# A branch over the last four chunks of three expert mixtures, and scatters moved to other places, in an eight-layer graph network

## The chip, the core and the metric

The kernel runs on one core of one Trainium2 chip. The core has five engines that run beside each other: PE (TensorE, matrix products), DVE (VectorE), ACT (ScalarE), POOL (GpSimd) and SP (SyncE, which here only starts transfers). PE's loading of weights is listed as PEld. Each engine works through its own instructions in order and waits on semaphores for the others. Data stand in on-chip memory as 128 partitions; PE's results go to a smaller accumulation memory and are copied out. Transfers to and from device memory (DMA) are started by SP, by ACT, or by POOL where the addresses come from an index list (an indirect DMA: a gather or a scatter of one row per partition).

The metric is the device time of one execution, in microseconds (us), median over several runs. A profile is taken of one execution, whose own time can differ a little from the median.

## The reference, cut to what matters

A state x of 3125 nodes by 256 features goes through eight steps; each adds its result to x, and each but the first works on a layer norm of x.

```
x = L0_gnn(x)                 # weighted sum over edges
x = x + L0_ffn(norm(x))       # mixture: 8 experts, hidden 512, top 2, relu
x = x + L1_gnn(norm(x))       # two attention passes over 50000 edges + self loops, 4 heads
x = x + L1_ffn(norm(x))       # mixture: 8 experts, hidden 256, top 2, gelu
x = x + L2_gnn(norm(x))       # weighted graph convolution and two dense layers
x = x + L2_ffn(norm(x))       # attention over 65536 edges, then 4 small experts, top 2
x = x + L3_gnn(norm(x))       # mean over neighbours, two layers
x = x + L3_ffn(norm(x))       # mixture: 8 experts, hidden 1024, top 2, gelu
```

The mixtures of L0, L1 and L3 are alike. For L0:

```
gate_logits = x_flat @ Wg + bg + bias
topk_vals, topk_idx = jax.lax.top_k(gate_logits, 2)
topk_w = jax.nn.softmax(topk_vals, axis=-1)
combine = (jax.nn.one_hot(topk_idx, 8) * topk_w[..., None]).sum(axis=1)
h = jax.nn.relu(jnp.einsum('td,edh->teh', x_flat, W1) + b1)
y = jnp.einsum('teh,ehd->ted', h, W2) + b2
out = jnp.einsum('ted,te->td', y, combine)
```

Only the two chosen experts of a node count, so 2 x 3125 = 6250 rows have to go through an expert. The attention passes of L1_gnn need, for each edge, the source node's projected row and a softmax over the edges of each target node. L2_ffn attends over another, larger edge list of its own.

## The kernel before, in words

The nodes are T = 25 tiles of 128; the state X stays on the chip. Most per-node work goes by groups of TG = 5 tiles. The steps are listed in FAST_STEPS (line 2523): `clear`, `r0_gnn`, `take_edges`, `middle`, `r2_gnn`, `r2_ffn`, `r3_gnn`, `r3_ffn`; `middle` (line 2325) holds L0's mixture, L1's attention and L1's mixture. A function `look` runs first and sorts the edges; it writes a flag that tells whether the fast way fits the data. All of the steps stand inside one branch on that flag (line 2534), the kernel's only one. Each engine loads the flag and branches for itself.

A planner orders the instructions of a stretch without branches (a basic block) on each engine, by program order and its own estimates of time. `in_order` (line 1919) takes that choice away: it chains all instructions of the engines named, in program order. Inside `middle` POOL is in order; in `attend` PE, DVE and ACT are too.

**A mixture** is `gated` (line 861). Before it the router has placed each node's row, for each of its two choices, into a device-memory buffer `regions`, which has one region for each expert (POOL scatters, line 831). `gated` counts each expert's rows, rounds up to chunks of CH = 256 rows (`gd_nch`), and takes the running sum over the experts (`gd_end`); the last entry of this sum is the number of chunks in use. Since no loop bound depends on the data, it runs as many chunks as could ever be needed, K = (2*3125 + 8*255)//256 = 32. A chunk k (lines 939 to 970) is: SP reads the chunk's expert and row from a table; loads the 256 rows (gx_xs), the expert's weights and its second bias; PE transposes the rows (L955); DVE copies them (L957); PE multiplies by the first weights (L962), ACT applies the function (L963); PE multiplies by the second weights (L933), one chunk later in program order; DVE adds the bias (L935); ACT stores 256 rows of results (L936) into `ff_results`. Chunks past the last one in use compute with expert 7 on rows that nobody reads. Afterwards (lines 972 to 978), for each tile and each of the two choices, POOL gathers the result rows (gb_y, through `gather`, L322) and DVE multiplies by the gate weight and adds into X (L977): 50 gathers, through 6 buffers.

**L1's attention** is `r1_gnn` (line 2255). It starts the next mixture's router (`mix_start`, line 712, with two small POOL iotas, L721 and L727, and DVE's `gd_zero`, L730), loads the head weights (`head_weights`, line 1905: the load hw_w at L1910, then DVE L1915 and L1916 twice each), and then, for each group of five tiles, normalises (`norm_group`: DVE L150, L156, L157; ACT L160; DVE L162, L163, five small ones and L170) and computes the `heads` (PE transposes, ACT L1942, PE L1946, ACT L1948, SP store of r_rows L1949, three small DVE operations). The second pass's weights use the same buffer, so their load waits until the last heads matmul has read the first ones. Then come two passes of `attend`. Each gathers 416 blocks of 128 edges' rows (POOL L322, ad_rows<-r_rows) and works on them; the second pass's gathers read what the first pass's last tiles stored.

**Scatters for L2_ffn.** The 65536 edges of L2_ffn are put in place by 512 POOL scatters (`own_send`, line 1733, instruction L1737: os_table<-os_rec), which are spread over the earlier steps wherever `own_send(n, after)` is called; each call issues the next n scatters, no earlier than the instruction `after`. The calls before: 4 after each of the first five buckets filled in L0_gnn (line 1474), two in each iteration of its main loop, 3 in each chunk of L0's and of L1's mixture (line 965; 96 each), 40 in `r1_gnn` after the head weights (line 2270), and `tail` (line 2297) with 6 a call, four calls at the end of each attention pass. What is left goes after L1's mixture. All 512 must be done before L2_ffn.

`rank_edges`, part of `look`, ranks the edges in their blocks; its PE matmuls are L1316, in three groups.

Of the kernel before, what the change touches and what calls it, by code (L numbers as in the profile page):

```python
# [61 lines left out]
class Net:  # L62
    def __init__(self, ctx, tc, a):
        self.ctx, self.tc, self.nc, self.a = ctx, tc, tc.nc, a
        self.turn = 0
# [27 lines left out]
    def clear(self):  # L93

        v = self.regions.rearrange("(q p r) d -> q p r d", p=P, r=8)
        for q in range(v.shape[0]):
            self.nc.sync.dma_start(v[q], self.zero[:, None, 0:D].to_broadcast([P, 8, D]))

# [762 lines left out]
    def gated(self, m, w1, b1, w2, b2, act, beside=None, send=0):  # L861
# [11 lines left out]
        K = (2 * N + E * (CH - 1)) // CH  # L873
        with tc.tile_pool(name="ge", bufs=1, side=m.side) as pool:
# [9 lines left out]
            nc.vector.tensor_tensor_scan(end, nch, nch, 0.0, OP.add, OP.max)  # L884
            kk = pool.tile([P, K], F32, name="gd_kk")
# [29 lines left out]
            with tc.tile_pool(name="gx_w", bufs=2) as wp, tc.tile_pool(name="gx_x", bufs=2) as xp, \  # L915
# [22 lines left out]
                last = None  # L938
                for k in range(K):

                    with tc.issue_after(prev.ins) if k else nullcontext():
                        e = nc.sync.value_load(ci[0:1, 0, k:k + 1], min_val=0, max_val=E - 1)
                        r = nc.sync.value_load(ci[0:1, 1, k:k + 1], min_val=0, max_val=E * RC - CH)
                    xs = xp.tile([P, CJ, D], F32, name="gx_xs")
                    nc.sync.dma_start(xs, regions[bass.ds(r, CH), :].rearrange("(j p) d -> p j d", p=P))
                    w1s = wp.tile([P, DC, F], F32, name="gx_w1")
                    nc.sync.dma_start(w1s, a[w1][bass.ds(e, 1), :, :].rearrange("o (c p) f -> p (o c) f", p=P))
                    w2s = wp.tile([P, FC, D], F32, name="gx_w2")
                    nc.sync.dma_start(w2s, a[w2][bass.ds(e, 1), :, :].rearrange("o (c p) d -> p (o c) d", p=P))
                    b2s = wp.tile([P, D], F32, name="gx_b2")  # L950
                    prev = nc.sync.dma_start(b2s, a[b2][bass.ds(e, 1), :].rearrange("o d -> (o d)").partition_broadcast(P))
                    pt = pt_.tile([P, DC, CH], F32, name="gx_pt")
                    for j in range(CJ):
                        for c in range(DC):
                            nc.tensor.transpose(pt[:, c, j * P:(j + 1) * P], xs[:, j, c * P:(c + 1) * P], self.ident)  # L955
                    xt = xp.tile([P, DC, CH], F32, name="gx_xt")
                    nc.vector.tensor_copy(xt, pt)  # L957
                    h = hp.tile([P, FC, CH], F32, name="gx_h")
                    for f in range(FC):
                        ps = pa_.tile([P, CH], F32, name="gx_pa")  # L960
                        for c in range(DC):
                            nc.tensor.matmul(ps, w1s[:, c, f * P:(f + 1) * P], xt[:, c, :], start=c == 0, stop=c == DC - 1)  # L962
                        done = nc.scalar.activation(h[:, f, :], ps, act, bias=bias1[:, f, k:k + 1])  # L963
                    if send:
                        self.own_send(send, done)
                    if last:
                        second(*last)
                    if beside and k == 1:
                        beside()
                    last = (k, h, w2s, b2s)  # L970
                second(*last)
            with tc.tile_pool(name="gb", bufs=6) as bp:
                for t in range(T):
                    for i in range(2):
                        y = bp.tile([P, D], F32, name="gb_y")
                        self.gather(y, results, at[i][:, t:t + 1])
                        nc.vector.scalar_tensor_tensor(self.X[:, t, :], y, w[i][:, t:t + 1], self.X[:, t, :],  # L977
                                                       op0=OP.mult, op1=OP.add)
# [179 lines left out]
class Fast(Net):  # L1158
# [114 lines left out]
    def rank_edges(self, over):  # L1273
# [4 lines left out]
        with tc.tile_pool(name="re", bufs=1) as pool, tc.tile_pool(name="re_ps", bufs=2, space=PSUM) as psp:  # L1278
# [31 lines left out]
            for i, (u, v, kb) in enumerate(((0, 12, KB), (12, T - 1, KB), (T - 1, T, KL))):  # L1310
# [3 lines left out]
                for j in range(2):  # L1314
                    for k in range(kb):
                        nc.tensor.matmul(ps[:, j, 0:n].rearrange("p (d s) -> p d s", s=T), both[:, j, :], hv[:, k],  # L1316
                                         start=k == 0, stop=k == kb - 1)
# [105 lines left out]
    def r0_gnn(self):  # L1423
# [12 lines left out]
        with ExitStack() as ctx:  # L1436
# [34 lines left out]
            for d in range(G):  # L1471
                for _ in self.fill_bucket((bp, psb), f5, d):
                    pass
                self.own_send(4, self.filled)
# [445 lines left out]
    def in_order(self, *engines):  # L1920

        tc, bb = self.tc, self.nc.cur_bb.bb
        n = len(bb.instructions)
        yield
        assert self.nc.cur_bb.bb is bb
        engines = [e.engine for e in engines]
        prev = {}
        for i in list(bb.instructions)[n:]:
            if i.engine in engines:
                if i.engine in prev:  # L1930
# [324 lines left out]
    def r1_gnn(self):  # L2255
# [7 lines left out]
        with tc.tile_pool(name="r1", bufs=1) as pool, tc.tile_pool(name="r1_ps", bufs=1, space=PSUM) as psp:  # L2263
# [33 lines left out]
            def tail(i):  # L2297
                self.own_send(6, i)
# [273 lines left out]
```

## Time and profile before

| what | value |
|---|---|
| median of 3 runs | 5167.04 us (5164.95 to 5167.39) |
| profiled execution, its own time | 5171.12 us |
| its span, first to last instruction | 5169.1 us |
| mean granted TensorE clock | 0.831 |
| busy: PE, DVE, ACT, POOL | 69%, 56%, 40%, 40% of the span |
| L0's chunks, 745 to 992 us of the span | 247 us |
| L0's 50 gathers, 996 to 1060 | 64 us |
| from there to the first attention gather, at 1132 | 72 us |
| L1's chunks, 2394 to 2556 | 162 us |
| L3's chunks, 4630 to 5095 | 465 us |

In the profile's timeline a row is: start in us from the beginning of the span, duration in us, engine, line of the kernel, operation, output<-inputs by the program's names, shapes, the count of merged instructions, and in brackets how long the engine had been idle before and what released it ("issue": nothing that the profile shows). "PE gx_pa L962 x32" in the chain is a piece of the chain that ended last, with its start and length. In "1024.0 KB" DMA rows and elsewhere buffer numbers are left out of names.

### The profile page before, as it was taken

How to read it: one execution, taken by the hardware profiler on the slowest of the kernel's cores; microseconds unless marked ns; L12 is line 12 of the kernel's file. 1: busy time of each engine (PE TensorE's matmuls, PEld its weight loads, DVE VectorE, ACT ScalarE, POOL GpSimd, SP SyncE). 2: the span in 40 equal slices, each digit the busy share in tenths (PEclk: the TensorE clock that was granted, in tenths of full speed). 3: DMA queues.
4: the chain of work that ended last, by engine and by line, in shares of the span. 5: the costliest groups of instructions: out<-in, count | busy, mean ns of one | idle time of the engine just before them, and what ended most of it. 6: DMA issues, size and time to landing. Idle time of an engine off the chain costs nothing.

```text
span 5169.1 us, 67040 instructions
## 1 busy us (share of the span) xinstructions
PE 3584.2 (69%) x21332; PEld 2847.3 (55%) x21332; DVE 2916.1 (56%) x9571; ACT 2087.0 (40%) x5715; POOL 2063.2 (40%) x2082
## 2 busy tenths in 40 slices
PE   1399969625666354554648876168786999979994
PEld 1399958524444243443537754035554788868883
DVE  7998842255666466663358874577747872231112
ACT  3466432116666467661129961023232331112220
POOL 0365443467776677775620000777700000120003
PEclk9699979866777677777969986578887999989997
DMA  1632237534554344434723311111100112225554
GB/s 55 206 109 103 99 123 234 174 89 136 142 142 125 97 133 130 135 99 132 205 74 115 115 57 45 34 31 35 33 1 25 68 68 76 92 103 193 193 192 135
DMA packets 345199, 562.37 MB, mean 109 GB/s; under 512 B 69987, under 2 KB 255719, under 8 KB 341637
## 3 DMA queue, kind: packets, MB, share of 16 engines
q1 hardware_dynamic: 229050, 373.88, 21.8%
q0 software_dynamic: 84032, 154.27, 11.7%
q10 hardware_dynamic: 31754, 29.84, 1.7%
q8 instruction: 172, 2.82, 0.2%
q14 instruction: 191, 1.56, 0.1%
HBM read 412.89 MB, written 145.37 MB: 108 GB/s over the span
## 4 chain that ended last, share of the span: by engine, by line
PE 44%; POOL 11%; DVE 9%; ACT 9%; issue 8%; DMA 5%; SPq 1%; DVEq 0%; ACTq 0%; POOLq 0%
POOL ad_rows L322 9%; PE gx_pa L962 7%; PE r_pa L1581 7%; PE gx_po L933 7%; PE ad_acc L2133 6%; ACT oo_y L1801 4%; PE q_a L2484 3%; PE q_o L2492 3%; PE r_o L1596 2%; DMA ad_rows<-r_rows,fa_gi 1%; DMA gb_y<-ff_results,gd_at 1%; ACT ad_rows L2123 1%; ACT oo_hp L1802 1%; ACT oo_h L1802 1%; DMA gx_xs<-regions 1%
## 5 line engine op out<-in xcount | busy, mean ns | idle before, releaser
L322 POOL DMA_INDIRECT ad_rows<-r_rows,fa_gi x832 | 823.3, 990 | 266.4 <-issue 241.3
L1737 POOL DMA_INDIRECT os_table<-os_rec,os_at x512 | 531.1, 1037 | 526.2 <-ACT gx_h L963 194.0
L322 POOL DMA_INDIRECT ad_rows<-q_rows,own_gi x416 | 402.6, 968 | 719.9 <-DMA q_rows<-q_hx 593.4
L2123 ACT ACTIVATE ad_rows<-ad_rows 128x64 f32<-128x64 f32 x2544 | 617.0, 334 | 1.6
L2133 PE MATMUL ad_acc<-ad_rows,ad_hd 128*128 128x260 f32 x1664 | 515.9, 464 | 3.3 <-ACT ad_rows L2123 2.4
L831 POOL DMA_INDIRECT regions<-gh_xn,gd_at x150 | 157.5, 1050 | 845.7 <-PE r_o L1596 624.4
L1581 PE MATMUL r_pa<-r_xs,r_cnt 128*128 128x257 bf16 x3750 | 467.7, 277 | 28.1 <-DVE r_xs L1357 14.2
L963 ACT ACTIVATE gx_h<-gx_pa,gx_bias 128x256 f32<-128x256 f32 x448 | 211.9, 473 | 671.2 <-PE gx_pa L962 642.6
L935 DVE TENSOR_TENSOR gx_ys<-gx_po,gx_b 128x256 f32<-128x256 f32 x192 | 80.6, 423 | 622.1 <-PE gx_po L933 600.8
L962 PE MATMUL gx_pa<-gx_xt,gx_w 128*128 128x256 f32 x1792 | 418.5, 388 | 6.8 <-DMA gx_w<-in_L_ffn_W 3.2
L933 PE MATMUL gx_po<-gx_w,gx_h 128*128 128x256 f32 x1792 | 419.5, 380 | 0.0
L1581 PEld LDWEIGHTS <-r_cnt 128*128 128x128 bf16 x3750 | 365.0, 99 | 84.9 <-issue 29.4
L2133 PEld LDWEIGHTS ad_acc<-ad_rows,ad_hd 128*128 128x128 f32 x1664 | 365.8, 232 | 68.9 <-ACT ad_rows L2123 5.4
L2036 PE MATMUL ad_pt<-ident,ad_e 128*4 128x128 f32 x75 | 26.6, 354 | 525.9 <-DVE ad_e L2033 396.0
L962 PEld LDWEIGHTS gx_pa<-gx_xt,gx_w 128*128 128x128 f32 x1792 | 336.6, 192 | 81.7 <-DVE gx_xt L957 21.5
L933 PEld LDWEIGHTS gx_po<-gx_w,gx_h 128*128 128x128 f32 x1792 | 331.2, 190 | 44.0 <-ACT gx_h L963 2.6
L322 POOL DMA_INDIRECT gb_y<-ff_results,gd_at x150 | 144.3, 962 | 526.9 <-DMA ff_results<-gx_ys 476.1
L2036 PEld LDWEIGHTS ad_pt<-ident,ad_e 128*4 128x4 f32 x75 | 6.1, 82 | 559.1 <-issue 527.4
L1462 PE MATMUL r_pa<-r_xn,r_wt 128*128 128x257 f32 x1250 | 298.1, 383 | 7.2 <-ACT r_wt L1497 5.9
L2360 PE MATMUL ss_sum<-r_xw,ss_wt 128*128 128x256 f32 x1250 | 292.0, 396 | 6.3 <-DMA ss_wt<-mats 6.3
L2360 PEld LDWEIGHTS ss_sum<-r_xw,ss_wt 128*128 128x128 f32 x1250 | 246.9, 199 | 42.3 <-issue 6.7
L1462 PEld LDWEIGHTS r_pa<-r_xn,r_wt 128*128 128x128 f32 x1250 | 228.4, 192 | 35.5 <-ACT r_wt L1497 6.5
(555 smaller groups left out, 6920.6 us busy)
## 6 DMA issues: line engine op xcount, KB each, us to landing
gx_w<-in_L_ffn_W SPq DMA_DIRECT2D x64, 1024.0 KB
mats<-r_wt SPq DMA_DIRECT2D x25, 1600.0 KB
ss_wt<-mats SPq DMA_DIRECT2D x25, 1600.0 KB
gx_w<-in_L_ffn_W SPq DMA_DIRECT2D x64, 512.0 KB
regions<-zero SPq DMA_DIRECT2D x26, 1024.0 KB
ad_rb<-fa_relT SPq DMA_DIRECT2D x48, 544.0 KB
gx_xs<-regions SPq DMA_DIRECT2D x96, 256.0 KB
ff_results<-gx_ys ACTq DMA_DIRECT2D x96, 256.0 KB
```

Source lines behind the costliest of these rows:

```text
L322: return self.nc.gpsimd.indirect_dma_start(out=out, out_offset=None, in_=table[:, :], in_offset=bass.IndirectOffsetOnAxis(ap=idx, axis=0))
L831: ins = nc.gpsimd.indirect_dma_start(out=self.regions[:, :], out_offset=bass.IndirectOffsetOnAxis(ap=m.at[i][:, t:t + 1], axis=0), in_=x, ...
L933: nc.tensor.matmul(po, h[:, f, j * P:(j + 1) * P], w2s[:, f, :], start=f == 0, stop=f == FC - 1)
L962: nc.tensor.matmul(ps, w1s[:, c, f * P:(f + 1) * P], xt[:, c, :], start=c == 0, stop=c == DC - 1)
L963: done = nc.scalar.activation(h[:, f, :], ps, act, bias=bias1[:, f, k:k + 1])
L1462: nc.tensor.matmul(pa, wt[:, i, :], xn[:, g * G + i, :], start=i == 0, stop=i == G - 1)
L1581: nc.tensor.matmul(pa, c[:, u, :], xs[i - 1][:, u, j, :], start=u == 0 and j == 0, stop=u == T - 1 and j == 2)
L1737: i = nc.gpsimd.indirect_dma_start(out=s.table[:, :], out_offset=bass.IndirectOffsetOnAxis(ap=s.at[:, c:c + 1], axis=0), in_=s.rec[:, c, : ...
L1801: nc.scalar.activation(y[:, k, :], self.iotab, AF.Abs, bias=minus[:, k:k + 1])
L2123: i = nc.scalar.activation(v, v, AF.Copy, scale=x.rt[:, k, W4 + h:W4 + h + 1])
L2133: nc.tensor.matmul(x.acc, lhs[:, k, :], rhs[:, k, :], start=i == 0, stop=i == x.kb - 1)
L2360: nc.tensor.matmul(sums[t], wt[:, d, :], rows[:, d, :], start=d == 0, stop=d == T - 1)
```

## The change

It does five things.

1. `gated` runs chunks 0 to KA - 1 = 27, with KA = 6250//256 + 8//2 = 28, as before. Chunks 28 to 31 stand in a branch that is taken when the number of chunks in use, loaded into a register of every engine, is above 28.
2. The result rows of these four chunks (1024 rows of 1 KB, 1 MB) are filled with zeros in each mixture, by one transfer that ACT starts in chunk 3.
3. The gathers of results become `mix_result`. For L0 they move into `r1_gnn`: for each group of five tiles ten gathers with their additions, then the group's norm and heads; ten gather buffers in place of six. The next mixture's `mix_start` comes after the heads.
4. Scatters: 7 after each of three matmul groups in `rank_edges` (new), 8 in place of 4 for each of the first five buckets, none in chunks 28 to 31, none of the 40 in `r1_gnn`, 9 in place of 6 in each call of the attention passes' tails.
5. `in_order` now works across basic blocks, by `resume`, `chain` and `branch`.

```
+    @contextmanager
+    def branch(self, cond):
+        for o in self.orders:
+            self.chain(o)
+        with self.tc.If(cond):
+            yield
+        for o in self.orders:
+            self.resume(o)
...
+        KA = (2 * N) // CH + E // 2
...
+            used = pool.tile([1, 1], I32, name="gd_used")
+            nc.vector.tensor_copy(used, end[0:1, E - 1:E])
...
-                    if send:
+                        if send and k < KA:
                             self.own_send(send, done)
...
+                        if k == 3:
+                            nc.scalar.dma_start(results[KA * CH:K * CH, :].rearrange("(q p) d -> p q d", p=P),
+                                                self.zero[:, None, 0:D].to_broadcast([P, (K - KA) * CJ, D]))
...
+                chunks(0, KA)
+                n = nc.values_load(used[0:1, 0:1], min_val=0, max_val=K)
+                with self.branch(n > KA):
+                    chunks(KA, K)
+        m.results = results
+        if tail:
             with tc.tile_pool(name="gb", bufs=6) as bp:
                 for t in range(T):
...
+                    self.mix_result(m, bp, t)
...
+    def mix_result(self, m, pool, t):
+        nc = self.nc
+        for i in range(2):
+            y = pool.tile([P, D], F32, name="gb_y")
+            self.gather(y, m.results, m.at[i][:, t:t + 1])
+            nc.vector.scalar_tensor_tensor(self.X[:, t, :], y, m.w[i][:, t:t + 1], self.X[:, t, :], op0=OP.mult, op1=OP.add)
...
+                self.own_send(7, done)
                 nc.vector.tensor_copy(start[:, u:v, :].rearrange("p d s -> p (d s)"), ps[:, 0, 0:n])
...
-                self.own_send(4, self.filled)
+                self.own_send(8, self.filled)
...
-            self.own_send(40)
             with tc.tile_pool(name="ln", bufs=2) as lp, tc.tile_pool(name="r1_xn", bufs=2) as xp, \
+                    tc.tile_pool(name="r1_h", bufs=3) as tp, tc.tile_pool(name="gb", bufs=10) as bp, \
                     tc.tile_pool(name="r1_p2", bufs=2, space=PSUM) as two:
                 for g in range(0, T, TG):
+                    for t in range(g, g + TG):
+                        self.mix_result(self.mix, bp, t)
                     xn = xp.tile([P, TG, D], F32, name="r1_xn")
                     self.norm_group(lp, xn, g)
...
+            self.mix_way.close()
+            self.mix_way = ExitStack()
+            m = self.mix = self.mix_start(self.mix_way, "L1_ffn_router_w", (), 8, probs=True, transpose=True, add=True)
...
-                self.own_send(6, i)
+                self.own_send(9, i)
```

## The prediction

> **What bounds the kernel now.** I read the page first, for the chain that ended last:
>
> ```profile
> PE 44%; POOL 11%; DVE 9%; ACT 9%; issue 8%; DMA 5%; SPq 1%; DVEq 0%; ACTq 0%; POOLq 0%
> POOL ad_rows L322 9%; PE gx_pa L962 7%; PE r_pa L1581 7%; PE gx_po L933 7%; PE ad_acc L2133 6%; ACT oo_y L1801 4%; PE q_a L2484 3%; PE q_o L2492 3%; PE r_o L1596 2%; DMA ad_rows<-r_rows,fa_gi 1%; DMA gb_y<-ff_results,gd_at 1%; ACT ad_rows L2123 1%; ACT oo_hp L1802 1%; ACT oo_h L1802 1%; DMA gx_xs<-regions 1%
> ```
>
> No one engine bounds it. The expert matmuls (L962 and L933, 14% together) and the attention gathers on POOL (L322, 9%) stand on the chain, and the change touches both. So I went stage by stage with a table of windows, one window for each loop over chunks (columns: busy us and instructions of PE, PEld, DVE, ACT, POOL; granted clock, DMA share, GB/s):
>
> ```profile
> 745.00:992.00 247.00, 245.70 (x1167) 205.96 (x1167) 57.74 (x147) 62.59 (x129) 93.24 (x96) 0.99 0.73 221
> 2394.00:2556.00 162.00, 138.30 (x640) 106.23 (x640) 46.64 (x96) 31.49 (x65) 90.84 (x94) 0.97 0.77 231
> 4630.00:5095.00 465.00, 464.10 (x2172) 399.95 (x2172) 48.40 (x95) 121.15 (x256) 0.00 (x0) 1.00 0.56 186
> ```
>
> PE is busy from end to end in L0 and L3, at a clock of 0.99 to 1.00; in L1 it is busy 138 of 162 us and waits for loads. Then the timeline around each edit.
>
> **Part 1: the skipped chunks, -107.9 us.** Each mixture sends two choices of 3125 nodes to 8 experts and runs K = 32 chunks of 256 rows. The branch runs chunks 28 to 31 only if more than 28 are used. That depends on the data, so I evaluated the reference's routing on its inputs. Rows per expert: L0 1325, 1693, 862, 239, 410, 1036, 474, 211; L1 522, 974, 433, 1344, 692, 713, 639, 933; L3 0, 1293, 416, 460, 1761, 84, 1429, 807. Rounded up to chunks each sums to 28 (L0: 6+7+4+1+2+5+2+1). 28 > 28 is false: all three are skipped. A count nearest to an upward flip is 1761, 31 rows below 1792; rounding won't move that. One chunk costs, by the starts of its transposes in L0 and of its L962 block in L3:
>
> ```profile
> 973.11 0.60 PE L955 MATMUL gx_pt<-ident,gx_xs 128*128 128x128 f32 x4
> 980.63 0.60 PE L955 MATMUL gx_pt<-ident,gx_xs 128*128 128x128 f32 x4
> ...
> 5060.21 7.11 PE gx_pa L962 x32
> 5067.32 6.04 PE gx_po L933 x28
> 5073.80 0.86 PE gx_po L933 x4
> 5074.66 7.11 PE gx_pa L962 x32
> ```
>
> 980.63 - 973.11 = 7.52 and 5074.66 - 5060.21 = 14.45. L1's first transposes start at 2394.53 and its last at 2549.84, 31 chunks later: 5.01. Four of each: 30.1 + 20.0 + 57.8 = 107.9.
>
> **Part 2: the branch itself, +1 us.** The only branch in the trace is the outer one, on the flag:
>
> ```profile
> 174.80 0.14 DVE L1243 TENSOR_SCALAR fa_flag<-fl_f 128x1 int32<-128x1 f32 x1
> 174.91 0.59 DVE L1343 TENSOR_TENSOR fa_rank<-re_r,re_r 128x416 bf16<-128x416 f32 x1
> 175.76 0.52 ACTq L921 DMA_DIRECT2D gx_b<-in_L_ffn_b  x1
> 175.82 0.14 POOL L721 IOTA gd_down<- 128x8 f32 x1 [135.19 <-DVE fa_rank L1343]
> ```
>
> From the flag written (174.94) to the first instruction behind it is 0.9 us, load and compare included, on the path that falls through; a jump over is not shown. The Trainium skill ("Runtime: NRT & Kernel Launch", section "Instruction fetch mechanics") speaks against the change: a taken branch whose target is outside the fetched window waits for a DMA fetch first. It prices none; the nearest small load here, hw_w below, takes 3.4 us. By the row three branches cost 2.7 us, by the rule 3 x (0.9 + 3.4) = 13 us, both uncovered. But after each mixture everybody waits for the last result's store: last y addition ends 992.24, first gather 995.76, first landed 998.63. POOL, which gathers, issues nothing inside the branch and gets there during these 3.5 us; DVE has 6 us, PE and ACT longer. So I take 1 us; ends 0 and 13.
>
> **Part 3: the zero fill, +4 us.** Each mixture now writes 1 MB of zeros at k = 3, on ACT's queue. At the 221 to 231 GB/s of the windows 1 MB is 4.5 us. L0 and L3 are bound by PE and prefetch, so it hides there; L1 waits for loads. I take L1's price, near 4; ends 0 and 14.
>
> **Part 4: L0's results into L1's norm and heads, -36 us.** Before, all 50 gathers come first, then norms, heads and 40 sends:
>
> ```profile
> 991.82 0.42 DVE L935 TENSOR_TENSOR gx_ys<-gx_po,gx_b 128x256 f32<-128x256 f32 x1 [1.30 <-PE gx_po L933]
> 995.76 0.99 POOL L322 DMA_INDIRECT gb_y<-ff_results,gd_at  x1 [5.71 <-issue]
> ...
> 1124.92 0.39 SPq L1910 DMA_DIRECT2D hw_w<-in_L_gnn_W  x1
> ...
> 1132.09 0.98 POOL L322 DMA_INDIRECT ad_rows<-r_rows,fa_gi  x1 [13.25 <-DVE hw_w L1916]
> ```
>
> First norm 1069.02; the 40 sends end 1118.84 and bind nothing. The second weight load hw_w goes when the last heads matmul has freed the buffer, and its L1915/L1916 (4 x 0.69 us) end the stretch: 7.2 us, which the change keeps. After: gathers keep their 1.25 us (995.76 to 1058.04), norm and heads run between. DVE needs per group 10 x 0.48 + 7.1 + 2.4 = 14.3 us against 12.5 of gathers; POOL and DVE go nearly level.
>
> Here a rule weighs. While a two-input DVE operation ran (L157, in L1's gathers beside the next norm), a gather of 0.95 us took
>
> ```profile
> 2582.26 1.83 POOL L322 DMA_INDIRECT gb_y<-ff_results,gd_at  x1 [0.30 <-issue]
> ```
>
> The Trainium skill ("SBUF — State Buffer", section "SBUF: two separate sides") says that the port pair shared by DVE and GpSimd is an exclusive lock: the loser blocks for the whole instruction. By it each L157 and L170 (1.49 us) could stop gathers wholly: 4 groups x 2 x 1.49 = 12 us; by the row 8 x 0.88 = 7. I take the row. So the last gather ends near 995.76 + 62.3 + 7 = 1065; it lands and is added 2.7 later (1068); the last group's norm takes 9 (1077), five heads 2.3 each as at 1118 to 1125 (11.5: 1088.5), the weight chain 7.2: 1096. 1132 - 1096 = 36. Bounds: 47 if nothing slows the gathers and heads overlap the norm; 15 if the planner puts additions ahead of norms in DVE's order (second rival).
>
> **Part 5: the sends (L1737), +29.5 in the tails, +5 before the flag.** One send is 0.97 + 0.30 = 1.27 us of POOL. Counts: 40 after L0 go; 21 appear in rank_edges, 20 in the bucket fill; 12 fewer in each of two mixtures (they leave with the skipped chunks); 12 more in each tail of attend. First tail, then second:
>
> ```profile
> 1693.58 1.00 POOL L1737 DMA_INDIRECT os_table<-os_rec,os_at  x1 [27.76 <-ACT ad_rows L2123]
> ...
> 1724.25 0.97 POOL L1737 DMA_INDIRECT os_table<-os_rec,os_at  x1 [0.30 <-issue]
> 1725.52 0.98 POOL L322 DMA_INDIRECT ad_rows<-r_rows,fa_gi  x1 [0.30 <-issue]
> ...
> 2342.00 0.97 POOL L1737 DMA_INDIRECT os_table<-os_rec,os_at  x1 [0.30 <-issue]
> 2343.28 0.97 POOL L831 DMA_INDIRECT regions<-gh_xn,gd_at  x1 [0.30 <-issue]
> ...
> 2347.14 1.49 DVE L157 TENSOR_TENSOR gh_xn<-X,ln_m 128x1280 f32<-128x1280 f32 x1 [14.83 <-DMA regions<-gh_xn,gd_at]
> ```
>
> POOL's order is fixed here. The second pass's first gather stands right behind the sends, 4.8 us after the last r_rows landed (1720.7), and POOL's gathers set the pass. 36 x 1.27 = 46 us from 1693.58, less the 1.15 us that the third call waited: +14.2. In the second tail the sends of rows to experts queue behind the 24, and the last norm waits 14.83 us for one; then come routing and the chunks: +12 x 1.27 = +15.3. Nothing hides either; lower bound 20 if the scheduler finds slack, upper 31.
>
> The 21 in rank_edges start as L1316's groups end (about 144, 149, 150), POOL being idle till 175.82. In numbers 27 us end at 171, before the flag. But DVE runs two-input operations over bf16 there (L1340 3.77 us at 145.59, L1333 5.67 at 150.22). If they block sends as the same rule says, three are out by 156 and 18 x 1.27 end at 179.5, 4.6 us past the flag; DVE's gd_zero waits for POOL's iota behind it, and DVE is busy 61 of the 62 us that follow. By the 1.83 row it would end near 172: 0. I take 5, ends 0 and 10. The 20 in the fill (193 to 238) leave a backlog of 25 us that POOL, busy 199 of the next 322 us, works off before anything waits: 0. Those in L0's and L1's chunks ride in POOL idle of 4 us a chunk in L0 and 1 to 3 in L1: 0.
>
> **Sum.** -107.9 + 1 + 4 - 36 + 29.5 + 5 = -104.4. The profiled execution took 5171.1 (span 5169.1 and 2.0 around it): 5066.7. It stood 4.1 above the median of the runs, so 5062.6; I predict **5062**.
>
> **Rivals.** (A) As summed, 0.66. (B) Norms don't interleave, 0.2: in L1's gathers the first group's norm, begun at 2574, was done only at
>
> ```profile
> 2628.15 1.48 DVE L170 TENSOR_TENSOR xn<-xn,ln_r 128x1280 f32<-128x1280 f32 x1
> ```
>
> after the last addition, since DVE's order held additions that waited for gathers ahead of it. If so here, part 4 yields 15 and the time is 5083. Against it: there the norms came later in program order, here norm and heads of a group come before the next group's gathers. (C) Branches stall, 0.1: fetches on every engine and lost preloading of the next stage's first operands, 10 us a branch, 5092. Against it: the cover of 3.5 to 6 us. (D) The other side, 0.04: branches taken. If the kernel counts 29 in all three, 107.9 is not saved, each adds a drain and refill of some 5 us, and the sum is 15 + 4 - 36 + 29.5 + 5 = +17: 5184, slower. It decides from the 29th chunk on; L3 and L0 must both flip to lose the gain. The routing's margins speak against it. This is also "the change doesn't do what it says".
>
> **Range.** 5032 holds part 4 at 47 and tails at 20 with nothing for parts 2 and 3; 5095 takes in B and C. 0.2% (10 us) is about what a measurement of this kernel tells from no change. Faster 0.95 (A, B, C less a little), same 0.01, slower 0.04 (D).
>
> **What would show it.** Windows of the chunk loops shorter by 30, 20 and 58 us; in each the next gather within 5 us of the last y addition. First ad_rows gather near 104 us after L0's last y addition, not 140; a first group's L170 before the third group's gathers. 36 sends back to back in each tail, with the first gather 14 and L157 15 us later against what precedes. POOL's sends past the flag or not. Wrong it is if any mixture shows 32 chunks, or if a tail's sends fit into a wait.

## The result and the profile after

The changed kernel takes **5074.99 us** (median of 4 runs, 5070.95 to 5084.68), against 5167.22 us for the kernel before measured beside it (4 runs, 5164.95 to 5171.31): a ratio of 0.9823, 95% interval [0.9806, 0.984]. That is 92 us less; 105 were forecast, and 5062 us. The profiled execution took 5071.18 us, its span 5069.4.

Both timelines are cut at the same events and subtracted. Each row runs from the event above it to its own (gd_kk is POOL's first operation in `gated`):

| stretch, ends at | before, us | after, us | difference |
|---|---|---|---|
| start, to L0's first chunk (first transposes) | 743.2 | 750.3 | +7.1 |
| L0's chunks, to the end of the last y addition | 249.1 | 219.8 | -29.3 |
| to L0's first result gather | 3.5 | 4.6 | +1.0 |
| L0's gathers, norm, heads, to the first attention gather | 136.3 | 104.4 | -32.0 |
| first attention pass, to its last gather | 532.8 | 529.8 | -2.9 |
| first tail, to the second pass's first gather | 60.7 | 78.0 | +17.4 |
| second pass, to its last gather | 573.0 | 570.6 | -2.4 |
| second tail, to gd_kk | 85.9 | 101.4 | +15.5 |
| to L1's first chunk | 10.1 | 10.2 | +0.1 |
| L1's chunks | 160.9 | 139.0 | -22.0 |
| to L1's first result gather | 3.9 | 9.0 | +5.1 |
| L1's gathers, all of L2, L3's gnn, to L3's first chunk | 2067.5 | 2065.0 | -2.5 |
| L3's chunks | 468.4 | 410.3 | -58.1 |
| to L3's first result gather | 3.4 | 6.7 | +3.3 |
| L3's gathers and the store | 70.5 | 70.5 | 0.0 |

The differences add up to the 99.7 us by which the spans differ (5169.1 - 5069.4).

The table of windows of the changed kernel, at the three chunk loops (busy us and instructions of PE, PEld, DVE, ACT, POOL; clock, DMA share, GB/s):

```profile
750.00:970.00 220.00, 217.24 (x1029) 180.88 (x1029) 53.13 (x140) 55.02 (x113) 81.58 (x84) 0.98 0.73 221
2369.00:2508.00 139.00, 121.19 (x560) 92.51 (x560) 40.92 (x84) 27.69 (x57) 79.90 (x83) 0.98 0.78 233
4582.00:4992.00 410.00, 407.90 (x1904) 351.33 (x1904) 42.98 (x84) 106.03 (x224) 0.00 (x0) 0.99 0.56 187
```

L1's 560 PE instructions are 28 chunks of 20, where there were 640: the bodies of the branches are skipped. The rates of 221, 233 and 187 GB/s are what they were within 2 GB/s.

L0's transition in the timeline of the changed kernel:

```profile
974.62 0.99 POOL L348 DMA_INDIRECT gb_y<-ff_results,gd_at  x1 [6.75 <-SPq L120]
...
1021.29 1.48 DVE L196 TENSOR_TENSOR r_xn<-r_xn,ln_r 128x1280 f32<-128x1280 f32 x1
...
1042.84 1.01 POOL L348 DMA_INDIRECT gb_y<-ff_results,gd_at  x1 [0.30 <-DVE ln_v L189]
...
1059.32 1.49 DVE L196 TENSOR_TENSOR r_xn<-r_xn,ln_r 128x1280 f32<-128x1280 f32 x1
...
1069.89 0.38 SPq L1958 DMA_DIRECT2D hw_w<-in_L_gnn_W  x1
...
1078.97 0.95 POOL L348 DMA_INDIRECT ad_rows<-r_rows,fa_gi  x1 [31.19 <-DVE hw_w L1964]
```

The norms finish while gathers still run (the second group's last operation is the row at 1021.29), and behind the last gather stand only the last group's norm and what is left of the heads. Then the two tails:

```profile
1639.98 1.00 POOL L1785 DMA_INDIRECT os_table<-os_rec,os_at  x1 [29.23 <-ACT ad_rows L2165]
...
1685.55 0.97 POOL L1785 DMA_INDIRECT os_table<-os_rec,os_at  x1 [0.30 <-issue]
1686.83 0.98 POOL L348 DMA_INDIRECT ad_rows<-r_rows,fa_gi  x1 [0.30 <-issue]
...
2317.49 0.97 POOL L857 DMA_INDIRECT regions<-gh_xn,gd_at  x1 [0.30 <-issue]
...
2321.47 1.49 DVE L183 TENSOR_TENSOR gh_xn<-X,ln_m 128x1280 f32<-128x1280 f32 x1 [30.25 <-DMA regions<-gh_xn,gd_at]
```

36 scatters stand back to back before the second pass, and the last norm of the second pass waits 30.25 us, where it waited 14.83, for a scatter of rows that stands behind the others.

In `look`, and at the flag:

```profile
145.49 3.78 DVE L1388 TENSOR_TENSOR re_eq<-re_eq,re_low 128x6936 bf16<-128x6936 bf16 x1
146.23 3.90 POOL L1785 DMA_INDIRECT os_table<-os_rec,os_at  x1 [0.30 <-issue]
...
150.11 5.68 DVE L1381 TENSOR_TENSOR re_q<-re_h,re_start 128x10200 bf16<-128x10200 bf16 x1
150.43 6.20 POOL L1785 DMA_INDIRECT os_table<-os_rec,os_at  x1 [0.30 <-issue]
156.94 0.97 POOL L1785 DMA_INDIRECT os_table<-os_rec,os_at  x1 [0.30 <-issue]
...
180.38 0.17 DVE L756 COPY gd_zero<-gd_base 128x8 f32<-128x8 f32 x1 [4.42 <-POOL gd_base L753]
```

The second and third scatter stretch from 0.97 to 3.90 and 6.20 us beside DVE's two-input operations of 3.78 and 5.68, and end 0.87 and 0.85 us after them; three are out by 157; and DVE's gd_zero comes at 180.4 where it came at 176.1.

What I had not seen coming are the start and the gaps of L1 and L3 (9.0 and 6.7 us, L3's is taken up with the run that has one chunk in the branch). L1's branch:

```profile
2507.06 0.86 DVE L965 TENSOR_TENSOR gx_ys<-gx_po,gx_b 128x256 f32<-128x256 f32 x2 [2.81 <-PE gx_po L963]
...
2511.66 0.37 SPq L1818 DMA_DIRECT2D fa_rec<-os_table  x1
2512.07 1.74 SPq L1820 DMA_DIRECT2D fa_rec<-os_table  x1
2516.02 0.38 DVE L1824 CAST ol_i<-fa_rec 128x416 int32<-128x416 f32 x1 [8.11 <-SPq L120]
...
2516.93 0.98 POOL L348 DMA_INDIRECT gb_y<-ff_results,gd_at  x1 [8.20 <-DVE ol_t L1825]
```

L120 is the branch. Two loads of the next layer stand just before it in SP's queue; they read the table that the scatters fill. SP's wait for the first (us in total, times, longest), and the listing of line 120 in this stretch (count, duration in ns, first and last start):

```profile
SPq L1818 <- DMA os_table<-os_rec,os_at: 10.1, 1, 10.1
```

```profile
L120 SPq EVENT_SEMAPHORE  x9: 17/17/17, 2514.4 to 2516.1; - x9
...
L120 SPq COMPARE_BRANCH  x1: 50/50/50, 2513.9 to 2513.9; - x1
```

SP stood until the 512th scatter had landed at 2511.6, issued the two loads, and only then reached the branch, at 2513.9, 5.9 us after the last y addition. Its steps over the branch raise the semaphores of the skipped transfers, two of them after these loads have landed (2515.6 and 2515.9). DVE's two operations on the loaded table follow, and at their end (2516.8) the first gather of L1's results.

### The profile page after: what moved, and what is told of

Its sections match the earlier page's. It is cut to its first block, busy times and chain, and to the rows that moved or that the text cites. A ratio compares the mean times of both kernels' runs of the same rounds, so it can differ in the third digit from the quotient of the medians.

```text
span 5069.4 us, 65672 instructions
## 1 busy us (share of the span) xinstructions
PE 3489.8 (69%) x20836; PEld 2764.9 (55%) x20836; DVE 2893.5 (57%) x9538; ACT 2061.0 (41%) x5659; POOL 2092.6 (41%) x2082
## 5 line engine op out<-in xcount | busy, mean ns | idle before, releaser
L1785 POOL DMA_INDIRECT os_table<-os_rec,os_at x512 | 559.4, 1093 | 560.8 <-ACT gx_h L994 172.8
L994 ACT ACTIVATE gx_h<-gx_pa,gx_bias 128x256 f32<-128x256 f32 x392 | 185.4, 473 | 586.8 <-PE gx_pa L993 568.3
L993 PE MATMUL gx_pa<-gx_xt,gx_w 128*128 128x256 f32 x1568 | 367.5, 389 | 6.7 <-DMA gx_w<-in_L_ffn_W 2.7
L963 PE MATMUL gx_po<-gx_w,gx_h 128*128 128x256 f32 x1568 | 366.5, 380 | 0.1
L993 PEld LDWEIGHTS gx_pa<-gx_xt,gx_w 128*128 128x128 f32 x1568 | 295.1, 193 | 72.7 <-DVE gx_xt L988 19.5
L963 PEld LDWEIGHTS gx_po<-gx_w,gx_h 128*128 128x128 f32 x1568 | 289.8, 190 | 38.5 <-ACT gx_h L994 2.4
```

The source lines that it names most:

```text
L963: nc.tensor.matmul(po, h[:, f, j * P:(j + 1) * P], w2s[:, f, :], start=f == 0, stop=f == FC - 1)
L1785: i = nc.gpsimd.indirect_dma_start(out=s.table[:, :], out_offset=bass.IndirectOffsetOnAxis(ap=s.at[:, c:c + 1], axis=0), in_=s.rec[:, c, : ...
```

## The experiments

All numbers of gaps and stretches are from the runs' profiles; ratios are to the kernel before, timed on the same chip.

**Tails of 6 again, 4 scatters in each of L0's chunks.**

```
-        self.gated(..., beside=self.fill_edges, send=3, tail=False)
+        self.gated(..., beside=self.fill_edges, send=4, tail=False)
...
-                self.own_send(9, i)
+                self.own_send(6, i)
```

> The changed kernel with 6 scatters in each tail call again, and L0's chunks carrying 4 each in place of 3 (112 in place of 84), so that all 512 are still placed. My theory: the 24 extra tail scatters stand on the chain at 1.27 us each and L0's chunks have 4 us of POOL idle each, so 31 us come off (about 5042 against the changed kernel's 5073): about 16 between the last gather of the first attention pass and the first of the second (78 to 62 us), 15 between the last gather of the second pass and gd_kk (101 to 86). Rival: ACT and PE set the ends of the tails and the scatters fill their waits: less than 5 us. Second rival: a fourth scatter slows L0's chunks beyond 7.5 us each, and takes back up to 28 x 1.3 = 36 us.

5041.61 us, ratio 0.9755 [0.9739, 0.9772]. The first tail went from 78.0 to 60.6, the second from 101.4 to 85.9, and L0's chunks took 219.7, as in the changed kernel. The 24 tail scatters stood on the chain with their whole length; 28 more in L0's chunks cost nothing.

**K = 28, without branch and zero fill.**

```
-        K = (2 * N + E * (CH - 1)) // CH
-        KA = (2 * N) // CH + E // 2
+        K = KA = (2 * N) // CH + E // 2
...
-                n = nc.values_load(used[0:1, 0:1], min_val=0, max_val=K)
-                with self.branch(n > KA):
-                    chunks(KA, K)
```

(The zero fill at k == 3 is taken out too.)

> K is 28 for good: no branch, no zero fill, chunks 28 to 31 do not exist. For these inputs nothing is left out, since 28 chunks are used. My theory: the branch cost 9.5 us in the changed kernel, seen as a later first result gather after the last y addition (4.55, 9.0 and 6.7 us in L0, L1, L3 against 3.5, 3.9 and 3.4 before), so the time falls by 9 to 10 us, these gaps go back to 3.4 to 3.9, and the scatter among runs (5071 to 5085) shrinks to some 5 us. Rival: the gaps have another cause than the branch (fewer chunks leave the last store less warm, a later POOL), and the time stays within 3 us.

5061.77 us, ratio 0.9798 [0.9782, 0.9814]. 13 us below the changed kernel; 9.3 of it are two gaps, L1's from 9.0 to 3.0 and L3's from 6.7 to 3.4. L0's stayed (4.6 and 4.9), but not for one reason: with the branch, 15 of the 16 pieces of L0's last store land within 2.3 us of the last y addition and one at 3.2; without it all of them land between 3.4 and 3.9. So what the branch costs in L0 stays open. The runs lie within 6 us.

**The zero fill without the branch.** As the changed kernel, but the last three lines of the diff above are taken out alone.

> As the changed kernel, zero fill included, but without the branch and without the code of chunks 28 to 31; for these inputs nothing is left out. It parts the zero fill from the branch. My theory: the zero fill is hidden (L1's 27 chunks took 5.0 us each with it), so this is within 1 us of the kernel with K = 28. Rival, as predicted: 4 us slower than that, in L1.

5065.39 us, ratio 0.9803 [0.9786, 0.9819]: 3.6 us above K = 28, by intervals that overlap. L1's chunks did not pay (136.9 us, 138.6 without the fill), so I looked for the transfers themselves. In the listing of the zero tile and of the result buffer (count, min/median/max duration of the issue in ns, first and last start in us), K = 28, then the changed kernel:

```profile
L98 SPq DMA_DIRECT2D regions<-zero x26: 660/3146/3917, 175.9 to 250.9; - x26
```

```profile
L98 SPq DMA_DIRECT2D regions<-zero x26: 659/3279/6510, 175.8 to 261.2; - x26
L1001 ACTq DMA_DIRECT2D ff_results<-zero x3: 366/409/666, 176.3 to 201.4; - x3
```

All three fills go out at 176 to 201 us, not in the chunks where the code has them: nothing held them there, and the planner moved them up, into the stretch in which SP clears 26 MB and the transfer engines are busy without a break (DMA share 1.00, 324 GB/s, from 176 to 238 in the kernel before). 3 MB at 324 GB/s are 9.7 us, and the clearing ends 10.3 us later. Of the thirteen changed kernels, the two without the fill (K = 28, and all 32 chunks) issue the last clearing at 250.9 (250.1 in the kernel before); the eleven with it do so at 260.8 to 261.6. L0's first chunk starts at 746.8 and 745.5 in the two, and at 748.0 to 753.6 in the five that differ from them only by the fill in this stretch: a mean of 749.9 against 746.2, 3.7 us.

**All 32 chunks, without branch and zero fill.**

```
-                chunks(0, KA)
+                chunks(0, K)
```

(and the branch and the fill are taken out)

> The changed kernel with chunks 28 to 31 always run, without branch and zero fill: part 1 undone alone. My theory: four chunks cost what their periods say, 30.1 + 20.0 + 57.8 = 107.9 us on top of the kernel with K = 28, so about 5171 to 5173, within 5 us of the kernel before. Rival: part of the chunks was covered by scatters or stores, and it is less than 90 us above K = 28.

5169.05 us, ratio 1.0006 [0.9997, 1.0015]: 107.3 above K = 28, where 107.9 were worked out. So without the chunks the other parts come to nothing together: tails against transition.

**Part 4 undone.** `r0_ffn` gathers its own results (tail=True, within mix_way), `mix_start` stands first in `r1_gnn` again, the ten gathers a group leave its loop; the 40 scatters are not put back.

> The changed kernel with part 4 undone: L0's 50 result gathers stand in its mixture again and L1's norm and heads come after them, without the 40 scatters. My theory: the whole of the 31 us between L0's last y addition and the first attention gather (140 before, 109 after) comes from the interleaving, so this is 28 to 32 us slower than the changed kernel. Rival: the 40 scatters slowed norm and heads through the port that POOL and DVE share, and their absence alone gives 8 us or more, so the loss is below 24.

5100.53 us, ratio 0.9882 [0.9866, 0.9899], 0.0059 or 30 us above the changed kernel. From the last y addition to the first attention gather 139.9 us, as in the kernel before (139.8), which had the 40 scatters there. They bound nothing.

**Loads of fa_rec away from L1's branch.**

```
-                self.own_send(7, done)
+                self.own_send((7, 7, 5)[i], done)
...
+        if tail and send:
+            self.own_send(1)
         if tail:
```

> In the changed kernel SP issues the two loads of fa_rec just before L1's branch, as the last of the 512 scatters is sent in chunk 27, and the first gather comes 9.0 us after the last y addition. Here one scatter stands behind the branch (19 in place of 21 in rank_edges), so that these loads, which need all 512, can only come behind it. My theory: on the way over a branch SP waits for every transfer in flight before POOL goes on, so the gap falls to 4 to 5 us, and the time by 4 to 5. Rival: the gap is the branch's own (fetching code), stays near 9, and the time stays.

The loads didn't move behind the branch but far ahead of it, to 2331.8, before the last scatters, so in this kernel they read a table that lacks those edges. Its time says nothing, its gap does: with no load in flight at the branch, L1's gap was 3.9 us.

**No scatters in rank_edges, 4 in each of L0's chunks.**

```
-                self.own_send(7, done)
```

> The changed kernel without the 21 scatters in rank_edges; L0's chunks carry 4 in place of 3. My theory: DVE's gd_zero comes at 176.1 again in place of 180.4 and L0's first chunk at 744 to 746 in place of 750.3, so 4 to 7 us come off. The first run above showed that 4 a chunk are hidden in L0. Rival: the time is set later, by the backlog of the bucket fill's 40 scatters, and 0 to 2 us come off.

5071.08 us, ratio 0.9823 [0.9806, 0.9839]: the changed kernel's own ratio. gd_zero came at 175.7, but L0's first chunk at 750.4. The view of ACT's waits between 237 and 330 us shows where the 4.7 us went (waited for; us in total, times, longest), this kernel:

```profile
ACT r_wt L1544 <- DMA mats<-r_wt: 6.3, 1, 6.3
```

and the changed kernel:

```profile
ACT r_wt L1545 <- DMA mats<-r_wt: 1.7, 1, 1.7
```

The first store of L0_gnn's matrices stands behind the clearing in SP's queue. ACT, and PE after it, wait for it; the clearing's end at 261 is fixed by the zeros, so who starts earlier waits longer. L1's gap was 3.5 here: with places for 7 scatters more the last of the 512 went out two chunks earlier, and the loads had landed before the last y addition.

**Branches taken.**

```
-                with self.branch(n > KA):
+                with self.branch(n > KA - 1):
```

> The changed kernel with the condition one chunk lower, so that all three branches are taken: the price of the branch where it doesn't save. My theory: the four chunks cost their 107.9 us, and each boundary a drain and a refill of the pipeline of 5 us and more (the first loads of chunk 28 wait behind the branch): 5075 + 108 + 3 x 5 - 9 = about 5190, slower than the kernel before by 15 to 35 us. Rival: SP runs ahead through the branch and the boundary costs nothing, so it ends near 5172.

The condition holds, so chunks 28 to 31 run and nothing is jumped over. 5185.57 us, ratio 1.0047 [1.0031, 1.0064]: 0.0041 or 21 us above the kernel that runs all 32 chunks without a branch. Against that kernel L0's chunks took 2.4 us longer, L1's 11.1, L3's 0.7 less. At L1's boundary PE stood still for the first rows of chunk 28:

```profile
2546.27 1.09 PE L986 MATMUL gx_pt<-ident,gx_xs 128*128 128x128 f32 x4 [9.60 <-DMA gx_xs<-regions]
```

The gaps to the first gather were 4.4, 3.8 and 4.0: without the jump L3's 6.7 isn't there.

**Only chunk 31 in each branch.**

```
-                    chunks(KA, K)
+                    chunks(K - 1, K)
```

> The changed kernel with only chunk 31 in each branch; chunks 28 to 30, which these inputs don't use, are left out, so that a branch is jumped over a quarter of the instructions. It asks what the later first gather of L3 is (6.4 to 6.9 us after the last y addition in every kernel that jumps, 4.0 where the branch is taken, 3.4 where there is none). My theory: each engine has to fetch the code behind a long jump; over one chunk the gap falls to 3.4 to 4.5, and in L1, where it comes from loads in flight, it stays near 9. Rival: going over a branch costs its 3 us whatever its length (SP's waits for all transfers before POOL goes on), and L3's gap stays at 6 to 7.

This run fell on a chip in a stretch of time when the kernel before took 5930 us there and attention gathers came at two thirds of their pace (74 in 150 us, where the changed kernel has 118), so only its own gaps and ratio are used: 0.9832 [0.9816, 0.9847]. L3's gap was 4.3 us, and 6.2 in the kernel beside it with four chunks in the branch. L1's was 3.4, which I had not expected: in this kernel the planner put the two loads behind the branch.

```profile
3022.35 0.97 POOL L1785 DMA_INDIRECT os_table<-os_rec,os_at  x1 [0.30 <-DVE gx_ys L965]
...
3025.02 0.38 SPq L1818 DMA_DIRECT2D fa_rec<-os_table  x1
3025.45 1.81 SPq L1820 DMA_DIRECT2D fa_rec<-os_table  x1
3025.93 0.98 POOL L348 DMA_INDIRECT gb_y<-ff_results,gd_at  x1 [2.61 <-issue]
```

Here they are in flight while POOL gathers: it was their place before the branch that cost. For L3 the DMA view of the 8 us around its end (packets and MB of the two instruction queues, share of 16 engines) shows in the changed kernel

```profile
q8 instruction: 3, 0.05, 4.2%
q14 instruction: 3, 0.02, 1.0%
```

and in the kernel with the fill and no branch

```profile
q14 instruction: 3, 0.02, 0.8%
q8 instruction: 1, 0.02, 0.7%
```

What the two more packets do stands in the traces' packets and landings. L3's last store lands in 16 pieces. In the changed kernel 14 of them are in by 4994.34, 2.2 us after the last y addition, and two land at 4996.38 and 4997.46. Two instruction packets of 16 KB were carried from 4992.81 to 4994.35 and from 4993.34 to 4995.95, and the packets of the two late pieces begin at 4994.33 and 4995.90, as these end. SP waits for the store on its way over the branch and passes on at 4997.48. The changed kernel, then the kernel with the fill and no branch:

```profile
4991.76 0.42 DVE L965 TENSOR_TENSOR gx_ys<-gx_po,gx_b 128x256 f32<-128x256 f32 x1 [3.03 <-PE gx_po L963]
...
4998.88 0.98 POOL L348 DMA_INDIRECT gb_y<-ff_results,gd_at  x1 [421.46 <-SPq L120]
```

```profile
4989.94 0.42 DVE L965 TENSOR_TENSOR gx_ys<-gx_po,gx_b 128x256 f32<-128x256 f32 x1 [3.03 <-PE gx_po L963]
...
4993.68 0.98 POOL L348 DMA_INDIRECT gb_y<-ff_results,gd_at  x1 [416.76 <-DMA ff_results<-gx_ys]
```

Over the kernels the last piece lands this long after the last y addition: 2.4 to 2.5 us without a branch, 2.9 where nothing is jumped over, 3.4 with a jump over one chunk, 4.7 to 5.4 over four (3.7 in the first run). The gather follows 1.4 us later over four chunks, 0.8 to 1.1 in the others.

One engine does stand at the branch itself, PE; its row in L3 is

```profile
L120 PEldq COMPARE_BRANCH  x1: 3307/3307/3307, 4988.8 to 4988.8; - x1
```

In L0 it took 3.71 us, over L1's shorter code 0.36, over one chunk 0.21 to 0.34, and 0.06 to 0.07 into chunk 28 where nothing is jumped over; the other engines' took 0.03 to 0.07. PE's ended at 4992.1, the last y addition at 4992.2, and POOL starts what comes next, so it isn't on the path.

**Scatters in L0's chunks, twice run.**

```
-                self.own_send(7, done)
+                self.own_send((7, 5, 0)[i], done)
...
-        self.gated(..., beside=self.fill_edges, send=3, tail=False)
+        self.gated(..., beside=self.fill_edges, send=5, tail=False)
...
-                self.own_send(9, i)
+                self.own_send(4, i)
```

> The changed kernel with its scatters placed where POOL is idle: 12 in rank_edges (7, 5, none), 8 a bucket, 5 in each of L0's chunks, 3 in each of L1's, 4 in each tail call: 520, so that the last goes out two chunks before L1's branch and the loads of fa_rec land ahead of it. My theory, from the first of these runs (5041.6): 8 fewer scatters in each tail, of which the first gives 4.8 us only (the rows of the second pass landed 4.8 us before its gathers) and the second 10; gd_zero at 176 in place of 180.4 gives 4; L1's gap at 3.5 gives 3: about 5020. Rival: five scatters a chunk (6.4 us of POOL in 7.5) hold up L0's gathers or slow its chunks, and it ends at 5030 or more; the tails' ends are set by ACT and PE, and nothing below 24 scatters counts.

Beside the run with one chunk in the branch, on the same slow footing: ratio 0.9819 [0.9806, 0.9833], no gain. L0's chunks took 254 us, and 220 in the other kernel. Windows of this kernel and of the other, from 800 to 950 us:

```profile
800.00:950.00 150.00, 132.37 (x611) 107.94 (x612) 34.71 (x99) 33.05 (x68) 80.67 (x84) 0.97 0.69 197
```

```profile
800.00:950.00 150.00, 148.51 (x716) 123.58 (x716) 38.53 (x105) 39.03 (x80) 56.39 (x58) 1.00 0.72 229
```

PE lost 16 of 150 us with more scatters in. The same kernel once more:

> The kernel with 5 scatters in each of L0's chunks and 4 in each tail call, once more. Its first run fell on a chip on which the kernel before takes 5930 us and the gathers of the attention passes come at half their pace; there L0's chunks took 254 us with five scatters each, and 220 with three in the run beside it. Theory: that was the chip, with its slow small transfers; where the kernel before takes 5160 to 5170 us, L0's chunks take 220 us and the ratio is near 0.972. Rival: five a chunk are too many on any chip: L0's chunks take 235 us or more, and the ratio is 0.976 or worse.

5031.03 us, ratio 0.9742 [0.9725, 0.9758], with the kernel before at 5163.95 on the same chip; L0's chunks took 221.0 us:

```profile
800.00:950.00 150.00, 148.79 (x709) 124.97 (x708) 31.34 (x65) 38.93 (x79) 95.97 (x100) 1.00 0.75 227
```

Five scatters a chunk cost about 1 us here, and 34 in the job in which gathers came at two thirds of their pace; why they cost so much there was not followed. The first tail became 59.4 us with 16 scatters, against 60.6 and 59.5 with 24 (the first run and the next one): below 24 other work ends it, and my 4.8 us there were at most 1.3. The second became 77.7, 8 less. The ratio is the lowest of all, 0.0081 or 42 us below the changed kernel's; its interval overlaps the first run's.

**Between the two: 4 in L0's chunks, 10 a bucket, 12 in rank_edges, 6 in the tails.**

> Between the first of these runs (tails of 6, L0's chunks of 4: a ratio of 0.9755 to the kernel before) and the one with 5 in each of L0's chunks: rank_edges sends 12, each bucket 10, L0's chunks 4, L1's 3, the tails 6 a call: 518, so that the last is out two chunks before L1's branch. My theory: gd_zero at 176 gives 4 us against the first run and L1's gap (6.3 there, 3.5 to 4 here) gives 3: a ratio near 0.974. Rival: neither is on the chain and the ratio is the first run's.

5042.48 us, ratio 0.9765 [0.9749, 0.9781]: that of the first run. L1's gap was 3.4 as forecast (6.3 in the first run), but ACT waited 7.7 us for the first matrix store, and L0's first chunk started at 751.4.

## Why the prediction was right or wrong

The direction was right, the mechanism (A) was right in all but one step, and the time lay within the range, 13 us above the figure. 8 of the 13 are a matter of executions: the sum gave 5066.7 for a profiled execution and the changed kernel's took 5071.2; but the profiled execution of before had stood 4.1 above its median, and that of after stands 3.8 below its own. The sum itself missed by 4.5:

| step | forecast | profile | what shows it |
|---|---|---|---|
| 1, chunks | -107.9 | -109.4 | 107.3 between K = 28 and 32 |
| 2, branches | +1 | +8.4 | gaps 9.0 and 6.7; 3.9 and 3.4 before; 3.0 to 3.4 without a branch |
| 3, zero fill | +4 | about +4 | medians 5065.4 and 5061.8; starts 749.9 and 746.2 |
| 4, transition | -36 | -31 | 139.8 against 108.9; undone: 30 us |
| 5, tails | +29.5 | +32.9 | tails of 6: 78.0 to 60.6, 101.4 to 85.9 |
| 5, flag | +5 | +3 | gd_zero +4.3; the start without fill 745.5 and 746.8, 743.2 before |
| rest | 0 | -7.8 | the two passes, L2 and L3's gnn |

That the sum missed by so little is partly luck. Steps 2, 4 and 5 were some 14 us too hopeful together and step 1 1.5 us too low; 7.8 us that nobody forecast, and that stay unexplained, took back over half.

**Step 1** came out as worked out. Its margin was misread: the count nearest to an upward flip is L0's 239, 17 rows below 256, not L3's 1761. Nothing flipped.

**Step 2 was the step that failed.** I had let the wait for the last store cover the branch, since POOL issues nothing in it. The sign I had named, a gather within 5 us of the last y addition, failed in L1 and L3. POOL has to wait for SP's steps over the branch, and SP can be late. In L1 it was late because it stood before the branch for two loads of another layer: 5.1 us more than the kernel before. The trace has the times (scatter landed 2511.6, branch 2513.9, loads landed 2515.9, DVE done 2516.8, gather 2516.9). Both halves are needed: in six kernels with a branch in which the loads had landed before the last y addition, or went out behind the branch, the gap was 3.4 to 4.0; in the two with 28 chunks and no branch the loads went out within 0.9 us of the first gather, and the gap was 3.0 and 3.3.

The other part is L3's 3.3 us. I had weighed the rule on code fetched behind a taken branch (the Trainium skill, "Runtime: NRT & Kernel Launch", section "Instruction fetch mechanics") at 3.4 us a branch, called it covered, and took the row. (In that rule's words a branch is taken when it jumps, here over the unused chunks.) PE's branch took 3.31 us in L3 and 3.71 in L0, which fits such a fetch, and it was covered as I had said. What I hadn't thought of is that fetched code and data get in each other's way: by the packets' times two instruction packets held up two of the last store's 16 pieces, for which POOL waits. (The trace doesn't name the engine that carried a packet.) That gave 2.8 us, and SP's passing on 0.5 more; that the sum is close to 3.4 is chance. In L0 what the branch costs stays open. Of rival (C), 10 us a branch, 8.4 us came true over all three.

**Step 3 had the size but not the place.** The fill cost L1 nothing; it was carried out at 176 to 201 us, where L0's fourth chunk comes at some 775, and lengthened the clearing.

**Step 4** was 5 us too good. The gathers took 69.2 us from the first start to the last end, 69.3 worked out. I had set the row against the rule on the shared port, but the rule held: every gather that met a norm's two-input operation ended 0.82 us after it, as here.

```profile
1034.47 1.48 DVE L196 TENSOR_TENSOR r_xn<-r_xn,ln_r 128x1280 f32<-128x1280 f32 x1
1034.52 2.26 POOL L348 DMA_INDIRECT gb_y<-ff_results,gd_at  x1 [0.30 <-DVE ln_m L176]
```

A gather loses only what is left of the operation when its turn comes, 1.3 us here and 0.4 to 0.9 in the others, so the 12 us of whole operations were too many. After the last gather the additions ended 3.6 us later (2.7 forecast), the last norm 13.4 (9), the heads 9.1 (11.5), the weights 9.1 (7.2). The norm was late because DVE still had the fourth group's last operation to do first (1.5 us), and because ACT came to its squares 2.9 us after their input was ready, behind copies for the heads. Rival (B) fell: the norms did interleave.

**Step 5.** Each tail scatter cost its 1.27 us. The first tail gave 3 more, since ACT released the first scatter 31.2 us after the last gather and not 28.7; in the other kernels with 36 scatters that tail took 74.4 to 78.0. The rule on the shared port carried the flag's step: scatters stood still for DVE's two-input operations, and gd_zero was 4.3 late, with 4.6 worked out. But that delay isn't worth 4.3: without it L0's first chunk starts no earlier (750.4, and 751.4 and 751.8 in the last two kernels), since the clearing's end comes next.

**The rest** I can't settle. Kernels with the same code there differ too: the first pass took 529.4 to 533.1 us, the second 570.6 to 575.6.

Rival (D), branches taken, was tried: 5185.57 us where 5184 was worked out, slower than before by 0.47%. Its 5 us for each drain and refill were 2.4, 11.1 and -0.7.

## What to carry to other kernels

Work that is only skipped by a branch is worth its whole period when the loop is bound by its engine, but look at what stands before the branch and what comes after it: a queue may be held up before it by transfers that have nothing to do with it, and code that a jump has fetched can hold up the data of the moment. A transfer that depends on nothing goes where the planner puts it, so its price is read from the stretch in which it runs, not from the line where it is written. Small operations that fill gaps belong into loops where their engine idles inside a period, and cost their full length at the seams between passes.

## What the runs showed of the hardware

A scatter on POOL of 0.97 us took 3.90 and 6.20 us while DVE ran two-input operations over 16-bit data of 3.78 and 5.68 us, ending 0.87 and 0.85 us after them, and 0.97 to 1.04 us beside DVE's reductions of 7.4 and 11.0 us, which have one input. A branch over four chunks took 3.3 to 3.8 us on PE in L0 and L3, 0.36 in L1, and 0.04 to 0.07 on the other engines. Beside two 16 KB instruction packets of 1.54 and 2.61 us, two of a store's 16 pieces landed 2.0 and 3.1 us behind the others. The same chip ran the kernel before at 5930 us in one job and at 5164 in another; in the slower one the attention gathers were the part that slowed, and there five scatters in a chunk, which cost about 1 us otherwise, cost 34 us.
